# Pairs of experts: reads issued a step behind their writes, rows gathered eight tiles ahead, slots listed in another order

## The chip, the cores and the metric

The kernel runs on one core of one Trainium2 chip. TensorE (PE) multiplies matrices, VectorE (DVE) and ScalarE (ACT) work elementwise, GpSimd (POOL) does indirect gathers and some elementwise work, SyncE (SP) issues transfers. The core has 16 DMA engines, which all its queues share. The metric is the device time of one execution in microseconds (us), as the median of several runs.

## The reference

The input x is (2, 2048, 512) in fp32. The reference is, cut to what matters:

```python
xn = layernorm(x)
s  = attention(xn)            # inner layernorm, causal, one head of 512, output projection, + xn
g  = silu(moe(xn))            # below
return x + s * g

def moe(x):                   # 4096 tokens, E = 8 experts, D = 512, H = 352
    scores = x @ gate_w.T + gate_b + bias
    top_scores, top_idx = top_k(scores, 2)
    gates = softmax(top_scores)
    comb = sum(one_hot(top_idx) * gates)
    h = silu(einsum('td,ehd->teh', x, w1) + b1)
    y = einsum('teh,edh->ted', h, w2) + b2
    return einsum('ted,te->td', y, comb)
```

The kernel computes the mixture for the two chosen experts of each token alone.

## The kernel before

The kernel has four stages. First the input is normalised block by block (eight blocks of 512 tokens) and projected for attention (0 to 261 us). Between these products the routing is computed: each token gets two *slots*, and slots are sorted by expert, in tiles of 128. Then the experts run tile by tile (261 to 660 us). Attention follows (to 1123 us), and it gathers each token's two expert outputs.

**The norm.** `norm_rows` writes normalised rows (`z_all`), and multiplies them on POOL by a ratio into `z_own` (L381). `turn_rows` reads the transposed copy back and stores `z_own` to DRAM as `zu_d` (L391), from which the experts gather. `put` (L869) hangs such calls behind numbered units of the projection; `key_sums` (L508, four POOL instructions) is called at fixed units too.

**The route.** `route` makes for each slot the token that fills it: one-hot tiles (`lane`, `slot_b`, L649) are multiplied on PE, and the result `toki` is the list of tokens, one column for each tile, one row for each partition.

**A tile's way through the experts.** NS is 68 tiles, of which 66 are always run; the first 60 belong to one expert each, the last are halves of two experts. In the order of the loop the first 7 tiles run singly, then 26 pairs of one expert each (`pair_step`), then the rest singly (`experts_step`). For every tile:

1. `gather` (POOL, L999): 128 rows of `zu_d` by `toki` into one of four buffers `xs`.
2. `turn`, `to_planes` (L108): `xs` is written to DRAM in four planes of 128 columns (`xs_d`, pieces of 512 bytes).
3. `read_back`, `from_planes` (L115): the planes are read back into one of four buffers `xring`, so that partition 32j + b of it holds the column piece j of the four rows 4b to 4b + 3.
4. `join`, `turn_blocks` (L119): VectorE transposes blocks of 32x32, which makes x transposed (`xT`); its output columns are written at a step of four.
5. `up` or, for a pair, `up_pair`: the product with w1. A pair uses seven half-size products (two matmuls each) and seven VectorE adds (L1179) into `hu`; its sums of x (`x_sums`, L1153) and of w1 (`w1_sums`) are made before.
6. `send_h`: `hu` is written in planes to `h_d` and read back into `huT`; `join_h` transposes it (`ht`) and applies Silu on ScalarE (L1205).
7. `down` (L1219): the product with w2; `keep_y` copies the result to `y` (two buffers) on ScalarE and SP stores it to `y_d` (L1228).

All engines run their instructions in program order, and the order is written by hand (`manual_schedule`). In `pair_step(i)` before, tile i + 4 is written out and read back in the same step: SP issues the write, and then the read-back when the write has landed. The same holds for h: it is written after `up_pair`, and its read-back is issued at the end of the same step. POOL's queue takes the writes and read-backs of the first seven row tiles, SP's all later ones. The last 32 columns of `hu` are padding; two memsets on POOL (L1061, L1062) set it before the first row tile is written.

Of the kernel before, what the change touches and what calls it, by code (L numbers as in the profile page):

```python
# [11 lines left out]
BF16 = mybir.dt.bfloat16  # L12
# [3 lines left out]
ALU = mybir.AluOpType  # L16
# [4 lines left out]
P = 128  # L21
# [5 lines left out]
def gated_attention_moe(  # L27
# [37 lines left out]
    ND = D // P  # L65
# [10 lines left out]
    FULL = (2 * NT * P - E * HALF) // P  # L76
    NS = -(-((2 * NT * P + E * (HALF - 1)) // HALF) // 2)
    NSP = NS + NS % 2
    NM = NS - 2
# [4 lines left out]
    order = list(range(2 * PAIRS, 2 * PAIRS + AHEAD_OF_PAIRS)) + list(range(2 * PAIRS))  # L84
    order += list(range(len(order), NS))
    paired = range(AHEAD_OF_PAIRS, AHEAD_OF_PAIRS + 2 * PAIRS)
# [8 lines left out]
    Q = P // 4  # L95
# [4 lines left out]
    y_d = dram.tile([NS * P, D], F32, name="y_d")  # L100
# [12 lines left out]
    def from_planes(queue, dst, src):  # L113

        queue.dma_start(out=dst, in_=src.rearrange("n j (b i) e -> (j b) n (i e)", i=4))  # L115

    def turn_blocks(dst, src):

        nc.vector.transpose(  # L119
            dst.rearrange("p c (b i) -> p i c b", i=4),  # L120
            src.rearrange("p (i c a) -> p i c a", i=4, a=Q),
        )

    y_rows = y_d.rearrange("(n p) d -> p n d", p=P)
# [60 lines left out]
    z_all = zp.tile([P, BT, D], F32, name="z_all", bufs=1)  # L185
    z_own = zp.tile([P, BT, D], F32, name="z_own", bufs=1)
# [132 lines left out]
    kts, zts, ratios, zuts, pgs = {}, {}, {}, {}, {}  # L319
    BY_TE = 1  # L320
# [30 lines left out]
    def norm_rows(b):  # L351
        xt = xin.pop(b)
        mv, va, rs = stats.pop(b)
        for t in range(BT):
            dst, src = z_all[:, t, :], xt[:, t, :]
            if b >= BY_TE:
                dst = dst.rearrange("p (j c a) -> p c j a", j=4, c=ND)
                src = src.rearrange("p (c j a) -> p c j a", j=4, c=ND)
            nc.vector.tensor_scalar(
                dst, src, mv[:, t, 0:1], rs[:, t, 1:2], ALU.subtract, ALU.mult  # L360
            )

        ratio = sm.tile([P, BT, 1], F32, name=f"ratio_{b}", tag="ratio", bufs=4)
        nc.vector.tensor_tensor(ratio, va[:, :, 1:2], rs[:, :, 1:2], ALU.mult)
        nc.vector.tensor_tensor(ratio, ratio, rs[:, :, 0:1], ALU.mult)  # L365
        nc.vector.tensor_copy(xscale[:, ts(b, BT)], rs[:, :, 0])
        nc.vector.scalar_tensor_tensor(
            xshift[:, ts(b, BT)], mv[:, :, 0], -1.0, rs[:, :, 0], ALU.mult, ALU.mult
        )
        ratios[b] = ratio  # L370
        if b >= BY_TE:
            to_planes(nc.sync, z_d[ts(b, BT)], z_all)
        for t in range(BT):
            dst, src = z_own[:, t, :], z_all[:, t, :]
            if b < BY_TE:
                dst = dst.rearrange("p (j c a) -> p c j a", j=4, c=ND)
                src = src.rearrange("p (c j a) -> p c j a", j=4, c=ND)
                own = ratio[:, t, :].unsqueeze(2).unsqueeze(3).to_broadcast([P, ND, 4, Q])
            else:
                own = ratio[:, t, :].to_broadcast([P, D])  # L380
            nc.gpsimd.tensor_tensor(dst, src, own, ALU.mult)  # L381
        if b < 2:
            turn_rows(b)
        if b < 2:
            load(b + 2)

    def turn_rows(b):
        if b >= BY_TE:
            zuts[b] = zup.tile([P, BT, D], F32, name=f"zuT_{b}", tag="zuT")
            from_planes(nc.sync, zuts[b], z_d[ts(b, BT)])  # L390
        nc.sync.dma_start(out=zu_rows[:, ts(b, BT), :], in_=z_own)  # L391

    def keys(b):
# [97 lines left out]
    LATE = 5  # L491
# [115 lines left out]
    def route():  # L607

        with ExitStack() as rt:
# [7 lines left out]
            for e in range(E):  # L617
# [5 lines left out]
                out=tri, in_=tri, compare_op=ALU.is_ge, fill=0.0,  # L623
# [5 lines left out]
            nc.gpsimd.memset(ones, 1.0)  # L629

            def counting(name, n, step=1, cm=0, dt=F32):
                i = rp.tile([P, n], I32, name=f"{name}_i")
                nc.gpsimd.iota(i, pattern=[[step, n]], base=0, channel_multiplier=cm)
                f = rp.tile([P, n], dt, name=name)
                nc.vector.tensor_copy(f, i)
                return f
# [9 lines left out]
            half = rp.tile([P, NJ], F32, name="half")  # L646
            nc.vector.tensor_copy(half, half_i)

            lane = counting("lane", P, dt=BF16)  # L649
            slot_b = counting("slot_b", NSP, dt=BF16)  # L650
            tok = [counting("row", NT, step=0, cm=1, dt=BF16), counting("tile", NT, dt=BF16)]

# [216 lines left out]
    def put(i, f, *args):  # L869
        between.setdefault(i, []).append((f, args))  # L870
# [5 lines left out]
    for b in range(1, NB):  # L876
        at = begin[b]
        put(at, keys, b)
        put(at + 3, both, b)
        put(at + (4 if b == NB - 1 else 7), keep_scores, b)  # L880
        if b > 1:

            before = begin[b - 1] if b > 2 else 0
            put(max(before - 1, 0), norm_stats, b)
            put(before + 1, norm_roots, b)
            put(before + 1, norm_rows, b)
            put(before + 3, turn_rows, b)
            if b + 2 < NB:

                put(before + 4, load, b + 2)  # L890
# [102 lines left out]
    xhp = st.enter_context(tc.tile_pool(name="xhp", bufs=1))  # L993
    xs = xsp.tile([P, 4, D], F32, name="xs")
    xring = xhp.tile([P, 4, D], F32, name="xring")
    FIRST = 6

    def gather(i):
        nc.gpsimd.indirect_dma_start(  # L999
            out=xs[:, (i + 1) % 4, :], out_offset=None, in_=zu_d,  # L1000
            in_offset=bass.IndirectOffsetOnAxis(ap=toki[:, order[i] : order[i] + 1], axis=0),
        )
# [49 lines left out]
    NHU = 4  # L1052
# [5 lines left out]

    hu = htp.tile([P, NHU, NH * P], F32, name="hu")
    huT = htp.tile([P, NHU, 4 * NH * Q], F32, name="huT")  # L1060
    nc.gpsimd.memset(hu[:, :, H:], 0.0)  # L1061
    nc.gpsimd.memset(hu[:, :, H : H + 1], 1.0)  # L1062
    xts, phs, hts, experts = {}, {}, {}, {}

    def slots(i, n=1):
# [4 lines left out]
    def turn(i, n=1):  # L1070
        queue = nc.gpsimd if i < paired.start else nc.sync
        to_planes(queue, xs_d[i : i + n], xs[:, slots(i, n), :])
        written.append((queue, xring[:, slots(i, n), :], xs_d[i : i + n]))
# [3 lines left out]
    def read_back(which, but=0):  # L1077
        while len(which) > but:
            from_planes(*which.pop(0))

    def join(i):
        xT = xtp.tile([P, ND, P], F32, name=f"xT_{i}", tag="xT")
        turn_blocks(xT, xring[:, (i + 1) % 4, :])
        xts[i] = xT

    def places(i):
# [112 lines left out]

    def join_h(i):  # L1200
        ht = hp.tile([P, NH, P], F32, name=f"ht_{i}", tag="ht")
        turn_blocks(ht, huT[:, (i + 1) % NHU, :])
        for c, (h0, hn) in enumerate(HCH):
            for at, j in places(i):
                nc.scalar.activation(  # L1205
                    ht[:hn, c, at], ht[:hn, c, at], AF.Silu, bias=b1sel[:hn, c, j : j + 1]
                )
        hts[i] = ht
# [16 lines left out]
    def keep_y(i, copy=nc.vector.tensor_copy):  # L1225
        y = yp.tile([P, D], F32, name=f"y_{i}", tag="y")
        copy(y, pys.pop(i))
        nc.sync.dma_start(out=y_rows[:, order[i], :], in_=y)  # L1228

    pys = {}  # L1230

# [2 lines left out]
    def experts_step(i):  # L1234


        def at(f, k):
            if 0 <= i + k < NM:
                f(i + k)

        if i != NM:
            at(copy_w2, -DOWN)
        if 0 <= i - DOWN - 1 < NM:
            keep_y(i - DOWN - 1, *[nc.scalar.copy] * (i < paired.start))
        at(turn, 4)
        if i + FIRST >= 4:
            at(gather, FIRST)
        read_back(written, i + 4 < NM)
        if i + 1 not in xts:
            at(join, 1)  # L1250

        for _ in range((2, 2, 1, 4, 3, 3, 1)[i] if 0 <= i < paired.start else 0):
            w1_sums(*sums_left.pop(0))
        if i < FULL:
            at(join_h, -2)
        at(up, 0)
        at(copy_w1, 1)
        at(send_h, 0)
        if i >= FULL:

            at(join_h, -2)
        at(down, -DOWN)
        read_back(written_h, i < NM)
# [4 lines left out]

    def pair_step(i):

        keep_y(i - DOWN - 1, nc.scalar.copy)
        read_back(written_h)
        read_back(written)
        turn(i + 4, 2)
        for k in range(2):
            gather(i + FIRST + k)
        if i > paired.start:
            join_x(i + 2)
        up_pair(i)
        if i == paired.start:  # L1280

            join_x(i + 2)
        read_back(written)
        send_h(i, 2)
        for k in range(2):
            join_h(i - 2 + k)
        down(i - DOWN)
        keep_y(i - DOWN, nc.scalar.copy)
        down(i - DOWN + 1)
        read_back(written_h)  # L1290
        if i + 2 in paired:
            x_sums(i + 2)

# [132 lines left out]
        mx, nm, pieces = scored[s]  # L1426
        nc.vector.tensor_reduce(nm, mx[:, : len(pieces)], AX.X, ALU.max, negate=True)

    for i in range(-5, 0):
        experts_step(i)  # L1430
        for _ in range(min(2, len(units) - 1) if i < -1 else len(units)):
            next(projected)
            if w2_left:
                load_w2(w2_left.pop(0))
# [534 lines left out]
```

## Time and profile before

| | |
|---|---|
| median of 3 runs | 1127.32 us (1126.23 to 1129.54) |
| profiled execution | 1124.87 us, its span 1123.2 us |
| PE busy | 1038.8 us (92% of the span) |
| VectorE busy | 721.0 us (64%) |
| ScalarE busy, POOL busy | 374.7 us (33%), 338.7 us (30%) |
| DMA | 224,500 packets, 261.78 MB, mean 233 GB/s |
| the 24 steps of pairs from 319.8 to 600.9 us | PE busy 242.18 us of 281.1; DMA share 0.81 |

A group of the profile is a source line with its engine and operands, the number of its instructions, their busy time and mean duration, and how long the engine stood idle just before them and for whom. A stretch of the trace is given with the busy time of each engine in it, the granted TensorE clock (1.00 is full speed) and the share of time in which the 16 DMA engines were busy. A DMA queue's row has packets, MB, and the time its packets took as a share of 16 engines. "A <- B" among the waits means that A stood until B was done. Line numbers are those of the kernel before.

### The profile page before, as it was taken

What the parts mean: (1) busy time and instruction counts of PE and PEld (TensorE: products, weight loads), DVE (VectorE), ACT (ScalarE), POOL (GpSimd) and SP (SyncE); (2) the same over time, 40 slices, a digit from 0 to 9 for tenths busy, and PEclk for the clock granted to TensorE, in tenths of its full rate; (3) what the DMA queues carried; (4) which work ended last, traced back from release to release, by engine and by line L of the source; (5) the groups of instructions that cost most, each with busy time, mean ns of one, the idle gap of its engine ahead of it and who ended that gap; (6) DMA issues with size and microseconds to landing.
All of it is one profiled execution on the core that took longest, in us unless ns stands there. A gap on an engine that the chain in (4) does not pass through costs nothing. (4 is left out here: it accounts for less than half of the span.)

```text
span 1123.2 us, 12952 instructions
## 1 busy us (share of the span) xinstructions
PE 1038.8 (92%) x3924; PEld 678.4 (60%) x3924; DVE 721.0 (64%) x1397; ACT 374.7 (33%) x751; POOL 338.7 (30%) x337
## 2 busy tenths in 40 slices
PE   9999899997689879888888899999999999999998
PEld 6878687853365655655555344667766544445677
DVE  6965846992666566565664355866767654677667
ACT  3434353321222223223222341223244544433341
POOL 3352552016111211111111102222334765743312
PEclk9999999999999999999999899999999999999999
DMA  8599888859677877787878865845476876865461
GB/s 292 197 308 347 298 291 317 278 173 326 203 233 246 237 241 243 240 258 226 266 246 241 248 210 201 264 135 188 163 228 204 305 227 212 259 191 189 144 211 38
DMA packets 224500, 261.78 MB, mean 233 GB/s; under 512 B 57384, under 2 KB 154408, under 8 KB 224432
## 3 DMA queue, kind: packets, MB, share of 16 engines
q1 hardware_dynamic: 167920, 189.36, 53.5%
q0 software_dynamic: 13920, 45.62, 11.8%
q10 hardware_dynamic: 42592, 25.96, 7.5%
q8 instruction: 34, 0.56, 0.2%
q14 instruction: 34, 0.28, 0.1%
HBM read 146.46 MB, written 114.43 MB: 232 GB/s over the span
## 5 line engine op out<-in xcount | busy, mean ns | idle before, releaser
L1219 PE MATMUL py<-arena,ht 128*128 (+3 forms) x396 | 189.2, 627 | 0.0
L999 POOL DMA_INDIRECT xs<-zu_d,toki x66 | 65.9, 999 | 336.5 <-DMA xs_d<-xs 270.5
L1205 ACT ACTIVATE ht<-ht,b1sel 128x128 f32<-128x128 f32 (+3 forms) x216 | 65.6, 380 | 265.1 <-DVE ht L119 265.1
L1336 PE MATMUL ps<-k,q 128*128 128x512 f32 (+3 forms) x416 | 143.0, 495 | 0.3 <-PEq L1487 0.3
L119 DVE STREAM_TRANSPOSE xT<-xring 128x512 f32<-128x512 f32 x66 | 67.1, 1077 | 100.9 <-DMA xring<-xs_d 100.9
L1219 PEld LDWEIGHTS py<-arena,ht 128*128 128x128 f32 (+3 forms) x396 | 76.8, 198 | 87.0 <-issue 85.7
L1706 POOL DMA_INDIRECT yg<-y_d,posi x64 | 69.3, 1083 | 187.4 <-DVE yg L1717 172.5
L1336 PEld LDWEIGHTS ps<-k,q 128*128 128x128 f32 x416 | 74.6, 190 | 67.2 <-issue 55.1
L119 DVE STREAM_TRANSPOSE ht<-huT 128x384 f32<-128x384 f32 x66 | 53.0, 863 | 57.6 <-DMA huT<-h_d 56.0
L1172 PE MATMUL p<-w1s,xT 128*128 x208 | 44.7, 340 | 41.0 <-DVE hu L1179 41.0
L119 DVE STREAM_TRANSPOSE pT<-puT 128x512 f32<-128x512 f32 (+2 forms) x74 | 67.9, 979 | 13.9 <-DMA puT<-p_d 13.7
L1563 PE MATMUL po<-v,pT 128*128 128x512 f32 x152 | 68.1, 594 | 2.9 <-DVE pT L119 2.5
L381 POOL TENSOR_TENSOR z_own<-z_all,ratio 128x512 f32<-128x512 f32 x32 | 41.7, 1332 | 89.8 <-DVE ratio L365 89.8
L1172 PEld LDWEIGHTS p<-w1s,xT 128*128 128x128 f32 x208 | 33.8, 198 | 47.7 <-DVE hu L1179 47.7
L1179 DVE TENSOR_TENSOR hu<-p,hu 128x176 f32<-128x176 f32 x182 | 54.6, 334 | 9.4 <-PE p L1172 2.8
L119 DVE STREAM_TRANSPOSE zT<-zuT 128x512 f32<-128x512 f32 x28 | 27.4, 1116 | 44.4 <-DMA zuT<-z_d 33.2
L1524 ACT ACTIVATE pT<-pT,nm 128x1024 f32<-128x1024 f32 x14 | 16.1, 1148 | 114.8 <-DVE ri L1687 65.3
L1524 ACT ACTIVATE pT<-ps,nm 128x512 f32<-128x512 f32 (+3 forms) x52 | 30.7, 589 | 70.9 <-DVE ri L1687 43.9
L1735 POOL TENSOR_TENSOR o<-o,yg 128x512 f32<-128x512 f32 x30 | 39.0, 1299 | 44.3 <-DVE o L1727 43.7
L1120 PE MATMUL ph<-w,xT 128*128 (+1 forms) x112 | 41.3, 517 | 11.2 <-DVE xT L119 6.3
L1727 DVE SCALAR_TENSOR_TENSOR o<-xo,xscale,o 128x512 f32<-128x512 f32 x30 | 30.2, 1015 | 32.5 <-ACT o L1724 26.3
L1563 PEld LDWEIGHTS po<-v,pT 128*128 128x128 f32 x152 | 28.4, 190 | 35.6 <-issue 34.1
(340 smaller groups left out, 2018.5 us busy)
## 6 DMA issues: line engine op xcount, KB each, us to landing
y_d<-y SPq DMA_DIRECT2D x66, 256.0 KB
xs_d<-xs SPq DMA_DIRECT2D x26, 512.0 KB
xring<-xs_d SPq DMA_DIRECT2D x26, 512.0 KB
h_d<-hu SPq DMA_DIRECT2D x26, 384.0 KB
huT<-h_d SPq DMA_DIRECT2D x26, 384.0 KB
zu_d<-z_own SPq DMA_DIRECT2D x8, 1024.0 KB
kt_d<-kT SPq DMA_DIRECT2D x16, 512.0 KB
q<-qt_d SPq DMA_DIRECT2D x32, 256.0 KB
```

Source lines behind the costliest of these rows:

```text
L119: nc.vector.transpose(dst.rearrange("p c (b i) -> p i c b", i=4), src.rearrange("p (i c a) -> p i c a", i=4, a=Q),)
L381: nc.gpsimd.tensor_tensor(dst, src, own, ALU.mult)
L999: nc.gpsimd.indirect_dma_start(out=xs[:, (i + 1) % 4, :], out_offset=None, in_=zu_d, in_offset=bass.IndirectOffsetOnAxis(ap=toki[:, order[ ...
L1120: nc.tensor.matmul(ph[at, :], lhsT=xT[:, c, at], rhs=rhs[k], start=(c == 0), stop=(c == ND - 1),)
L1172: nc.tensor.matmul(ps, lhsT=x[:, c], rhs=y(c).rearrange("p o h -> p (o h)"), start=(c == 0), stop=(c == ND // 2 - 1),)
L1179: nc.vector.tensor_tensor(out, x, y, ALU.add)
L1205: nc.scalar.activation(ht[:hn, c, at], ht[:hn, c, at], AF.Silu, bias=b1sel[:hn, c, j : j + 1])
L1219: nc.tensor.matmul(py[at, :], lhsT=ht[:k, c, at], rhs=rhs[n], start=(c == 0), stop=(c == NH - 1),)
L1336: nc.tensor.matmul(ps[:, :w], lhsT=aqs[seq[s] // 2][:, c, ts(t % 2, P)], rhs=aks[first + j][:, c, :w], start=(c == 0), stop=(c == ND - 1),)
L1524: nc.scalar.activation(dst, src, AF.Exp, bias=nm, accum_out=rs[:, j : j + 1])
L1563: nc.tensor.matmul(dst, lhsT=turned[s][:, ts(k, P)], rhs=avs[first + k // BT][:, k % BT, cols], start=(start and k == k0), stop=(k == k1 - 1),
L1706: nc.gpsimd.indirect_dma_start(out=y, out_offset=None, in_=y_d, in_offset=bass.IndirectOffsetOnAxis(ap=posi[k][:, n : n + 1], axis=0),)
```

## The change

- **Reads behind writes.** `pair_step` now begins with the read-backs: that of the pair of row tiles written in the step before, and that of the h written in the step before. The read-backs after `up_pair` and at the end of the step are gone. Rows are written out six tiles ahead (`SENT`) instead of four, and gathered eight ahead (`FIRST`) instead of six. The single steps read rows back before they write the next tile. The loop before the first tile starts one step earlier.
- **Slots in the planes' order.** `lane` is listed so that partition 4a + i of a gathered tile holds slot a + 32i of the tile. `turn_blocks` then writes its columns in contiguous runs ("i b"), and x transposed still has its slots in order. For the 60 tiles of one expert h is turned the same way, so that the rows of y come out permuted, and the store of y puts them back: its destination is 4 x 32 rows of 512 where it was 128 rows.
- **Padding later.** The two memsets of the padding stand behind the POOL work of the last step ahead of the first tile.
- **The norm's own rows.** The multiplication on POOL and the store of `z_own` are functions of their own. For all blocks but the sixth (b = LATE = 5) they are called where they were; for that block the multiplication comes two units later, behind `key_sums(3)`, and the store two units later.

```diff
-    def turn_blocks(dst, src):
+    def turn_blocks(dst, src, rows="b i"):
...
-            dst.rearrange("p c (b i) -> p i c b", i=4),
+            dst.rearrange(f"p c ({rows}) -> p i c b", i=4),
...
             put(before + 3, turn_rows, b)
+            put(before + (3 if b == LATE else 1), own_rows, b)
+            put(before + (5 if b == LATE else 3), store_rows, b)
...
-            lane = counting("lane", P, dt=BF16)
+            lane = counting("lane", [[1, Q], [Q, 4]], dt=BF16)
...
-    FIRST = 6
+    FIRST, SENT = 8, 6
...
-    nc.gpsimd.memset(hu[:, :, H:], 0.0)
-    nc.gpsimd.memset(hu[:, :, H : H + 1], 1.0)
...
-        turn_blocks(xT, xring[:, (i + 1) % 4, :])
+        turn_blocks(xT, xring[:, (i + 1) % 4, :], "i b")
...
-        turn_blocks(ht, huT[:, (i + 1) % NHU, :])
+        turn_blocks(ht, huT[:, (i + 1) % NHU, :], "i b" if i < FULL else "b i")
...
-        nc.sync.dma_start(out=y_rows[:, order[i], :], in_=y)
+        rows = y_d[ts(order[i], P)]
+        nc.sync.dma_start(
+            out=rows.rearrange("(b i) d -> i b d", i=4) if i < FULL else rows, in_=y
+        )
...
-        at(turn, 4)
+        if i == paired.stop:
+            read_back(written_h)
+        read_back(written, i < paired.stop + 2)
+        at(turn, SENT)
         if i + FIRST >= 4:
             at(gather, FIRST)
-        read_back(written, i + 4 < NM)
...
     def pair_step(i):
 
+        read_back(written)
+        read_back(written_h)
         keep_y(i - DOWN - 1, nc.scalar.copy)
-        read_back(written_h)
-        read_back(written)
-        turn(i + 4, 2)
-        for k in range(2):
-            gather(i + FIRST + k)
+        turn(i + SENT, 2)
+        for k in range(i + FIRST, min(i + FIRST + 2, NM)):
+            gather(k)
...
             join_x(i + 2)
-        read_back(written)
         send_h(i, 2)
...
         down(i - DOWN + 1)
-        read_back(written_h)
...
-    for i in range(-5, 0):
+    for i in range(-SENT, 0):
         experts_step(i)
+        if i == -1:
+            nc.gpsimd.memset(hu[:, :, H:], 0.0)
+            nc.gpsimd.memset(hu[:, :, H : H + 1], 1.0)
```

More of the change, by code (lines that the diff above doesn't have):

```diff
@@ L372, in norm_rows @@
             to_planes(nc.sync, z_d[ts(b, BT)], z_all)
[L373 to L381, printed above, removed]
         if b < 2:
+            own_rows(b)
             turn_rows(b)
+            store_rows(b)
         if b < 2:
@@ L390, in turn_rows, with own_rows, store_rows @@
             from_planes(nc.sync, zuts[b], z_d[ts(b, BT)])
+    def own_rows(b):
+        for t in range(BT):
+            dst, src = z_own[:, t, :], z_all[:, t, :]
+            if b < BY_TE:
+                dst = dst.rearrange("p (j c a) -> p c j a", j=4, c=ND)
+                src = src.rearrange("p (c j a) -> p c j a", j=4, c=ND)
+                own = ratios[b][:, t, :].unsqueeze(2).unsqueeze(3).to_broadcast([P, ND, 4, Q])
+            else:
+                own = ratios[b][:, t, :].to_broadcast([P, D])
+            nc.gpsimd.tensor_tensor(dst, src, own, ALU.mult)
+    def store_rows(b):
         nc.sync.dma_start(out=zu_rows[:, ts(b, BT), :], in_=z_own)
@@ L631, in counting @@
             def counting(name, n, step=1, cm=0, dt=F32):
+                pattern = n if isinstance(n, list) else [[step, n]]
+                n = math.prod(size for _, size in pattern)
                 i = rp.tile([P, n], I32, name=f"{name}_i")
-                nc.gpsimd.iota(i, pattern=[[step, n]], base=0, channel_multiplier=cm)
+                nc.gpsimd.iota(i, pattern=pattern, base=0, channel_multiplier=cm)
                 f = rp.tile([P, n], dt, name=name)
```

## The prediction, made before the result was known

> **What bounds the kernel now.** I read the windows by stage first, then the waits of the stage that the change rewrites, then its DMA. The steady paired stage runs from the first product of the second pair (319.8 us) to that of the last (600.9 us): 24 equal steps in 281.1 us, 11.71 us each.
>
> ```profile
> 319.80:600.90 281.10, 242.18 (x962) 160.17 (x961) 166.79 (x361) 75.19 (x217) 45.78 (x47) 0.96 0.81 247
> ```
>
> The columns are length, busy us (and count) of PE, PEld, DVE, ACT, POOL, granted clock, DMA share, GB/s. PE is busy 242.18/24 = 10.09 us of each step, so 1.62 us per step is PE idle; the DMA engines are busy 81% of it. Who waits for whom in that stage (total us, times, longest):
>
> ```profile
> POOL xs L999 <- DMA xs_d<-xs: 236.2, 25, 10.8
> ...
> DVE xT L119 <- DMA xring<-xs_d: 79.8, 24, 4.5
> ...
> PE p L1172 <- DVE hu L1179: 38.9, 22, 3.1
> ```
> ```profile
> SPq L115 <- DMA xs_d<-xs: 111.1, 24, 5.6
> SPq L115 <- DMA h_d<-hu: 97.2, 24, 5.5
> ```
>
> The chain is plain. SP issues the write of a pair's rows and then stands 111.1/24 = 4.6 us for it before the read-back; the read-back lands late for the VectorE transposes (3.3 us per step); the adds L1179 are queued behind those transposes, and PE's last product waits for them, 38.9/24 = 1.62 us, which is all of PE's idle time. POOL's 236 us is slack, since nothing waits for it. Attention behind this stage is bound by PE (98% busy from 800 to 900 us), so what the paired stage loses or gains arrives at the end in full.
>
> **The change, part by part.** *Reads behind writes.* Read-backs move to the start of the next step and rows are written out six tiles ahead, not four. SP no longer stands for the write, and the 3.3 us on VectorE and 1.62 us on PE go. Taken alone that leaves PE's 10.09 us against 9.5 us of DMA (below), so a step of 10.1: 25 x (10.1 - 11.71) = -40 us (25 steps, since the first is set otherwise, below).
>
> *The store of y.* Its destination is now 4 x 32 rows instead of 128. No row of the trace shows a store of that shape. First its present price, from a stretch in which only y is stored:
>
> ```profile
> DMA packets 476, 0.88 MB, mean 98 GB/s; under 512 B 48, under 2 KB 48, under 8 KB 475
> ...
> q1 hardware_dynamic: 475, 0.87, 25.2%
> ```
>
> This is 671 to 680 us: 25.2% of 16 engines x 9 us = 36.3 us of engine time for 0.87 MB, that is 3.3 stores of 0.262 MB: 10.9 us of engine time each, or 0.68 us on each of 16 engines. Now the rule that speaks against this change: the Trainium skill, "DMA: Bandwidth & Descriptors", section "Why a DMA increments its semaphore by 16 and not by 1", says that a DMA runs on the largest number of engines, up to 16, that divides the slowest dimension of both sides, and on the lowest-numbered ones. With 128 and 4 that is four, always the same. This case's trace supports the counting: SP issues 560 DMAs, and its queue holds 8,840 four-byte completion packets. 552 x 16 + 8 x 1 = 8,840, and exactly eight of the DMAs (L989) have one row. By the rule a store costs 10.9/4 = 2.73 us on each of four engines; by the present row 0.68 us on all. The stretch of the 24 steps:
>
> ```profile
> q1 hardware_dynamic: 69852, 56.56, 69.3%
> q0 software_dynamic: 3840, 12.59, 11.6%
> ...
> y_d<-y SPq DMA_DIRECT2D x48, 256.0 KB
> ```
>
> With 0.3% of instruction fetch, 81.2% of 11.71 us is 9.51 us per engine and step. Two stores are 1.37 us of it, and become 5.47 us on four engines: 9.51 - 1.37 + 5.47 = 13.6 us. That is the upper end, because mean packet times hold the long reads, some of which run side by side on an engine. With the median packet times of the trace (ns: 22 for the 384 B pieces of h_d, 27 for the 512 B pieces of xs_d, 65 for huT, 84 for the 2 KB rows of xring and y, 160 for the gathers) an engine of the four does per step 64 x 22 + 64 x 27 + 16 x 65 + 16 x 84 + 64 x 84 + 8 x 160 ns, 12.2 us, and with the completions 12.25, the lower end. I take the middle, 12.9 us, because both ends describe the same traffic. This exceeds PE's 10.1, so four engines set the step: 25 x (12.9 - 11.71) = **+30 us** (+13.5 to +47). By the 16-engine row it would be the -40 above.
>
> The waits that this adds: SP issues the read of h only when the write of h has landed, with a store of y and the next write of rows queued behind it, and ScalarE's copy into y waits for the store two before (two buffers), with the copy of the first product and the Silus behind it. Both feed the same loaded engines later; they make no step longer than the engines' own sum as long as work is queued there, and SP has a whole step of it queued.
>
> *Slot order and transposes.* The permuted list (L649) costs the same iota (0.23 us) in the route. The transposes write contiguously instead of at a step of four. Now:
>
> ```profile
> L119 DVE STREAM_TRANSPOSE xT<-xring 128x512 f32<-128x512 f32 x66 | 67.1, 1077 | 100.9 <-DMA xring<-xs_d 100.9
> ```
>
> The bounds are 1.08 us as now and 0.68 us, what a TENSOR_TENSOR of 128x512 takes (L423). VectorE is busy 166.79/24 = 6.9 us of a step, so PE and DMA hide either value; I take no change. Were VectorE the bound, the difference would be up to 1.4 us a step.
>
> *Start of the experts.* The padding's memsets stood 7.5 us on POOL, ahead of the first write of rows:
>
> ```profile
> 252.82 0.21 POOL L1061 MEMSET hu<- 128x128 f32 x1 [7.53 <-DVE share L859]
> ```
>
> The first row tiles come 5 to 7 us earlier, and PE's idle 4.84 us before the first expert (265.61) goes. This does not reach the first pair, though. It waits for the sums of x, which stand behind the fifth ht transpose on VectorE; those transposes start at 281.54, 287.60, 293.85, 300.08 and 306.48, one per 6.2 us: transpose 0.86, Silus 0.99, copy of hu 0.43, issues 0.8, landing some 3.1. That ring is not edited; its head hangs on the weight loads ahead on SP (last at 270.30, waiting for stores of v). I take -1 us (-3 to +2, the latter if the first 4-engine stores cross it). Gathering eight ahead adds no instruction, only moves 66 of 1.0 us on an idle POOL.
>
> *Block 5 of the norm.* Its own-scaled rows (4 x 1.25 us on POOL) move behind the key sums of block 3, for which PE waits once:
>
> ```profile
> PE bank_d L554 <- POOL arena L513: 3.3, 1, 3.3
> ```
>
> PE has no other gap there: -3 us. The 1 MB store of those rows also moves two units later on SP, past the four loads of x and the store of q. Those loads then land sooner and the rows are gathered over 100 us later. Its price lies in z_own: block 6's rows (136.29 us) need that store landed. Issued near 129 with some 6.5 us to land, it is at the edge: 0 to +3 us, so this part is -3.3 to 0.
>
> *Behind the pairs* the tiles still storing through four engines share them with the loads of k; 614 to 660 us already has a DMA share of 0.86. Six such stores add 2 us each on four engines; PE's work hides most of it: +2 us (0 to +6).
>
> **Sum.** +30 - 1 - 3 + 2 = +28 us on the profiled execution's 1124.87 us (span 1123.2 and 1.67 around it): 1152.9. The median of the runs, 1127.32, lies 2.45 above that execution: 1155.
>
> **Rivals.** (1) The store still runs on 16 engines. For it: the same 128 rows of 2 KB move, and every large DMA of the trace does. Against it: the completion count, which follows the number of rows. Then PE bounds: -40 - 1 - 3 = -44, so 1083. This is the faster side. It is decided by one number: below about 11.7 us of work per step on the busiest engine the stage gains, and that is reached if a store has at least six to eight engines. (2) Four engines, but their packets overlap so well that they finish a step in the present 11.7 us (84 ns for 2 KB would have to fall towards 75): the lost and won waits cancel, and -4 from the start remains: 1123. (3) Four engines, with mean packet times or pauses in their queues (SP held by the h write while they run dry): 13.6 us a step, some 1172 to 1182.
>
> **How the numbers follow.** Four engines as the bound (with rival 3 as its upper part): 0.83, own range 1134 to 1182 (13.5 - 3 - 3.3 = +7, and 47 + 2 + 6 = +55). Rival 1: 0.12. Rival 2: 0.05. The range leaves out rival 1 and the far tails: 1120 to 1182. The three runs spread by 0.3%, about what can be told from no change. Faster: rival 1, half of rival 2 and the lowest tail, 0.15; same 0.04; slower 0.81.
>
> **What the profile after would show.** If right: DMA packets in all fall by 60 stores x 12 completions = 720 from 224,500; a store of y takes longer to land than its present 3.5 to 7.7 us; steps of about 12.9 us; DMA share in the stage falls to about 0.74 while the step grows; SP's waits for xs_d are gone, and PE's waits move to what the late h or x reads feed. If the memset mattered more, the first pair starts well before 301.9 us. The prediction is wrong if the packet count is unchanged, or if a step falls under 11 us.

## The result, and the profile after

The changed kernel takes 1224.55 us (median of 3 runs, 1221.99 to 1226.66) against 1127.32 before: a ratio of 1.086, 95% interval 1.082 to 1.090. Slower, as forecast, but by 97 us where +28 was forecast, and 43 us above the upper end of the range.

Where the time went, by the starts of PE's products (us, from the two traces):

| stretch | before | after | difference | forecast |
|---|---|---|---|---|
| start to the first product of the second pair | 319.8 | 323.3 | +3.4 | -4 |
| 24 steps of pairs | 281.1 (11.71 each) | 364.3 (15.18 each) | +83.2 | +28.6 |
| last pair to the end of the span | 522.4 | 535.3 | +12.9 | +2, and +1.2 for a 25th step |
| span | 1123.2 | 1222.8 | +99.6 | |

The paired stage once more, now of the kernel after. The columns are those of the prediction's first line: length, busy us (and count) of PE, PEld, DVE, ACT, POOL, granted clock, DMA share, GB/s.

```profile
323.27:687.53 364.26, 278.25 (x961) 202.90 (x960) 140.97 (x353) 70.13 (x209) 45.47 (x48) 0.84 0.66 189
```

PE is busy for 76% of the stretch where it was busy for 86%, and the DMA engines for 0.66 instead of 0.81. So this is not a stage in which the sixteen are full. The waits of the same stretch (total us, times, longest), first the engines', then SP's queue from 319.8 to 688.6 us:

```profile
DVE ht L119 <- DMA huT<-h_d: 172.8, 23, 8.6
...
PE p L1180 <- DVE xs L1161: 86.0, 23, 4.9
```
```profile
SPq L1237 <- ACT y L1235: 120.1, 24, 9.2
SPq L115 <- DMA h_d<-hu: 22.6, 24, 1.2
SPq L115 <- DMA xs_d<-xs: 12.1, 24, 0.7
SPq L108 <- DVE hu L1187: 9.8, 13, 1.2
```

SP's wait for the write of rows has gone from 4.6 us a step to 0.5, as the prediction said. In its place SP stands 120.1/24 = 5.0 us for ScalarE's copy into y. VectorE waits 172.8/23 = 7.5 us a step for the read of h (26.6 us in all before), and PE 86.0/23 = 3.7 us for the sums of x, which follow the h transposes on VectorE.

The packets of the whole kernel after:

```profile
DMA packets 223780, 261.77 MB, mean 214 GB/s; under 512 B 56664, under 2 KB 153688, under 8 KB 223712
```

224,500 - 223,780 = 720, that is 60 stores x 12 completions: by this count the stores run on four engines. What a step looks like on SP (start, us it took, operation):

```profile
446.00 0.52 SPq L1237 DMA_DIRECT2D y_d<-y  x1
447.02 0.36 SPq L115 DMA_DIRECT2D xring<-xs_d  x1
448.39 0.36 SPq L115 DMA_DIRECT2D huT<-h_d  x1
448.85 0.54 SPq L1237 DMA_DIRECT2D y_d<-y  x1
449.50 0.96 SPq L108 DMA_DIRECT2D xs_d<-xs  x1
451.39 6.23 SPq L108 DMA_DIRECT2D h_d<-hu  x1
461.38 0.52 SPq L1237 DMA_DIRECT2D y_d<-y  x1
```

Two things are to be seen. The order is store, two read-backs, store, two writes, so every read and every write is issued behind a store that uses the same four engines. And SP took 6.2 us to issue the write of h (median of the stage 6.5), for which it took 0.46 us before:

```profile
448.63 0.46 SPq L108 DMA_DIRECT2D h_d<-hu  x1
```

The transfers of that step, in 40 slices of 0.4 us from 447 to 463 us (upper line: busy tenths of the sixteen engines):

```profile
DMA  2356199853679467989999986544999821113113
GB/s 61 52 45 36 46 297 369 323 210 77 116 116 160 145 195 268 312 310 275 289 320 352 357 296 239 197 156 145 305 296 286 236 88 60 44 44 84 42 51 66
```

At both ends of the step there are some 2 to 3 us with mostly 36 to 66 GB/s. In the trace's packet records 2 KB packets on one engine start 80 ns apart, 1.5 KB ones 61, 512 B ones 23.4 and 384 B ones 18.7, which is 20 to 26 GB/s an engine: about two engines work there, and fourteen have nothing. From 460.6 us on most packets are 512 B ones, 34 in each 0.4 us, and then 384 B ones, some 42, which is two engines' pace: the last pieces of the two writes that SP waits for.

The transposes, last:

```profile
L119 DVE STREAM_TRANSPOSE ht<-huT 128x384 f32<-128x384 f32 x66 | 36.7, 587 | 239.5 <-DMA huT<-h_d 239.5
...
L119 DVE STREAM_TRANSPOSE xT<-xring 128x512 f32<-128x512 f32 x66 | 43.4, 687 | 13.3 <-DMA xring<-xs_d 13.3
```

1077 has become 687 ns and 863 has become 587, by writing contiguously.

### The profile page after: what moved, and what is told of

It is laid out like the page before. It is cut to its first block, busy times and chain, and to the rows that moved or that the text cites. A ratio compares the mean times of both kernels' runs of the same rounds, so it can differ in the third digit from the quotient of the medians.

```text
span 1222.8 us, 12954 instructions
## 1 busy us (share of the span) xinstructions
PE 1078.5 (88%) x3924; PEld 724.2 (59%) x3924; DVE 688.7 (56%) x1397; ACT 371.9 (30%) x751; POOL 335.9 (27%) x337
## 2 busy tenths in 40 slices
DMA packets 223780, 261.77 MB, mean 214 GB/s; under 512 B 56664, under 2 KB 153688, under 8 KB 223712
## 5 line engine op out<-in xcount | busy, mean ns | idle before, releaser
L1227 PE MATMUL py<-arena,ht 128*128 (+3 forms) x396 | 179.2, 598 | 1.6 <-ACT ht L1213 1.6
L119 DVE STREAM_TRANSPOSE ht<-huT 128x384 f32<-128x384 f32 x66 | 36.7, 587 | 239.5 <-DMA huT<-h_d 239.5
L1180 PE MATMUL p<-w1s,xs 128*128 x208 | 69.5, 483 | 96.9 <-DVE xs L1161 96.9
L1227 PEld LDWEIGHTS py<-arena,ht 128*128 128x128 f32 (+3 forms) x396 | 72.1, 187 | 79.0 <-issue 75.6
L1180 PEld LDWEIGHTS p<-w1s,xs 128*128 128x128 f32 x208 | 56.0, 310 | 103.6 <-DVE xs L1161 94.5
L1187 DVE TENSOR_TENSOR hu<-p,hu 128x176 f32<-128x176 f32 x182 | 59.1, 339 | 47.6 <-PE p L1180 44.5
L1180 PE MATMUL p<-w1s,xT 128*128 x208 | 56.9, 413 | 0.0
L119 DVE STREAM_TRANSPOSE zT<-zuT 128x512 f32<-128x512 f32 x28 | 27.3, 1110 | 45.4 <-DMA zuT<-z_d 40.7
L119 DVE STREAM_TRANSPOSE xT<-xring 128x512 f32<-128x512 f32 x66 | 43.4, 687 | 13.3 <-DMA xring<-xs_d 13.3
```

The lines of the kernel that those rows point to most:

```text
L119: nc.vector.transpose(dst.rearrange(f"p c ({rows}) -> p i c b", i=4), src.rearrange("p (i c a) -> p i c a", i=4, a=Q),)
L1180: nc.tensor.matmul(ps, lhsT=x[:, c], rhs=y(c).rearrange("p o h -> p (o h)"), start=(c == 0), stop=(c == ND // 2 - 1),)
L1187: nc.vector.tensor_tensor(out, x, y, ALU.add)
L1227: nc.tensor.matmul(py[at, :], lhsT=ht[:k, c, at], rhs=rhs[n], start=(c == 0), stop=(c == NH - 1),)
```

## The experiments

Every ratio is to the kernel before, run on the same chip beside it. "Step" is the median distance between SP's issues of two reads of xring in the trace; by that measure it is 11.59 us before and 15.29 after. The kernel before had medians of 1125 to 1132 us on the chips used, so a difference in us between two other kernels is good to some us only.

The expectations weigh explanations by name. *Work*: the engines that carry a store have more to move than a step has time for. *Ring*, or *turn*: a step is a closed chain of waits (read of h, transposes, Silus, copy, store, read of h). *Form*: a strided store is dear in itself. *Queue*: transfers that somebody waits for are issued behind stores. In y_16, y_8, y_2, late_8 and turn_two_2 the rows of y land in another order within their tile, so these kernels leave out the reference's row order; the bytes moved are the same.

| kernel | engines per store | us | ratio (95%) | step, us |
|---|---|---|---|---|
| before | 16 | 1127.32 | 1 | 11.59 |
| after | 4 | 1224.55 | 1.086 (1.082 to 1.090) | 15.29 |
| y_rows | 16, plain rows | 1105.78 | 0.980 (0.975 to 0.986) | 10.47 |
| y_16 | 16 | 1126.26 | 0.999 (0.997 to 1.001) | 11.48 |
| y_8 | 8 | 1172.28 | 1.038 (1.034 to 1.041) | 13.53 |
| y_2 | 2 | 1270.79 | 1.126 (1.122 to 1.130) | 16.50 |
| before_y4 | 4 | 1217.41 | 1.081 (1.076 to 1.086) | 15.01 |
| late_store | 4 | 1205.14 | 1.071 (1.067 to 1.076) | 14.46 |
| late_8 | 8 | 1126.68 | 1.002 (1.000 to 1.003) | 11.78 |
| rows_late | 16, plain rows | 1114.83 | 0.990 (0.987 to 0.993) | 11.19 |
| act_y | 4 | 1196.00 | 1.060 (1.054 to 1.066) | 14.40 |
| act_rows | 16, plain rows | 1099.80 | 0.980 (0.974 to 0.985) | 10.22 |
| turn_two | 4 | 1229.68 | 1.087 (1.079 to 1.094) | 15.37 |
| turn_two_2 | 2 | 1273.08 | 1.126 (1.118 to 1.133) | 16.50 |
| y_last | 4 | 1156.75 | 1.027 (1.023 to 1.031) | 12.60 |
| last_rows | 16, plain rows | 1087.88 | 0.965 (0.960 to 0.970) | 9.78 |
| bufs_4 | 4 | 1224.16 | 1.089 (1.083 to 1.095) | 15.25 |

### How many engines a store has

Four kernels differ from the changed one in the store's shape alone. y_rows turns h back to the rows' own order, so that a store is 128 plain rows:

```
-        turn_blocks(ht, huT[:, (i + 1) % NHU, :], "i b" if i < FULL else "b i")
+        turn_blocks(ht, huT[:, (i + 1) % NHU, :])
...
-        nc.sync.dma_start(
-            out=rows.rearrange("(b i) d -> i b d", i=4) if i < FULL else rows, in_=y
-        )
+        nc.sync.dma_start(out=rows, in_=y)
```

> The change with one part undone: h is turned in its old order, so y comes out in order and is stored to 128 rows as before. Theory of work (the engines that carry a store of y do more per step than anything else; a step after the change is 15.18 us, of which two stores on four engines are 5.45 us): two stores on 16 engines are 1.36 us, the DMA falls to 9.5 to 11.1 us a step and PE's 10.1 us becomes the bound: 1083 to 1125 us, and PE's waits for x or h mostly gone. Theory of the ring (the read of h is issued behind a store whose copy waits for the Silus of the read before; only half of the stores lie in it): the step falls by 2.04 us, 1172 us.

y_16, y_8 and y_2 change one figure (here y_16):

```
-            out=rows.rearrange("(b i) d -> i b d", i=4) if i < FULL else rows, in_=y
+            out=rows.rearrange("(b i) d -> i b d", i=16) if i < FULL else rows, in_=y
```

> The store keeps its strided, three-dimensional destination, but with 16 x 8 rows instead of 4 x 32 (so rows of y land in another order within their tile, and the output differs). Theory of work: as with 128 rows, 1083 to 1125 us. Theory of the ring: 1172 us. Theory of the form (a strided destination is dear in itself, whatever its outermost size): 1225 us, no change.

> The destination has 8 x 16 rows (order within the tile differs, and so the output). Completion packets rise by 60 x 4 = 240 against the changed kernel. Theory of work: two stores on eight engines are 2.73 us a step, 15.18 - 2.73 = 12.45 us, some 1157 us. Theory of the ring: half of that, 1190 us. Theory of the form: 1225 us.

> The destination has 2 x 64 rows (order within the tile differs, and so the output). Theory of work: two stores on two engines are 10.9 us a step, 15.18 + 5.45 = 20.6 us, some 1360 us. Theory of the ring: half of that, 1292 us. Theory of the form: 1225 us.

The packet counts are 224,500 for 16, 224,020 for 8, 223,780 for 4 and 223,660 for 2, so by the completions the number of engines follows i. y_rows lies in the range that *work* gave, y_16 just above it, y_8 between *work* (1157) and *ring* (1190), y_2 under both (1360 and 1292). The store's shape explains the whole loss: without it the change is 2% faster than before. Two parts can be told apart. The number of engines costs 1224.55 - 1126.26 = 98 us from 16 to 4. The strided form costs 1126.26 - 1105.78 = 20 us at the same 16 engines and the same bytes, although y_rows has the slower transposes of h; SP took 0.53 us to issue it where the plain one took 0.33.

The sizes fit no simple theory. By count, a store's work per engine doubles with each halving, but the losses are 46, 52 and 46 us. With two engines, one step takes 16.50 us, and two engines' work at the packets' pace is 128 x 80 ns for two stores and 64 x 18.7 + 64 x 23.4 + 16 x 61 + 16 x 80 + 8 x 160 ns = 6.2 us for the rest, 16.5 us: that fits two engines that are simply full. With four, the same count gives 5.1 + 6.2 = 11.4 us, and the step is 15.3. Something beside the work counts.

### The store alone, in the kernel before

```
-        turn_blocks(ht, huT[:, (i + 1) % NHU, :])
+        turn_blocks(ht, huT[:, (i + 1) % NHU, :], "i b" if i < FULL else "b i")
...
-        nc.sync.dma_start(out=y_rows[:, order[i], :], in_=y)
+        rows = y_d[ts(order[i], P)]
+        nc.sync.dma_start(
+            out=rows.rearrange("(b i) d -> i b d", i=4) if i < FULL else rows, in_=y
+        )
```

> The kernel before with nothing but its y store changed to 4 x 32 rows on four engines (and the transposes of h to the slot order that this needs). In it the write of a pair's rows and the read-backs stand behind its y stores too, and SP stands for that write. Work theory (engines' own sum, as in the prediction): 12.25 to 13.6 us a step, 1141 to 1175 us. Ring theory: two stores stand in the serial turn of the step and each is some 2 us longer on four engines, 25 x 4.1 = 102 us more: some 1230 us, about what the whole change costs, so the new order of the read-backs would not be to blame for the loss, only the store.

before_y4 takes 1217.41 us, nearer to *ring* (1230) than to *work* (at most 1175), so the store by itself costs the old kernel nearly what the whole change costs. Its SP waits, from 400 to 580 us (12 steps), and its issues of the write of h (min, median and max in ns):

```profile
SPq L115 <- DMA xs_d<-xs: 94.1, 12, 8.1
SPq L115 <- DMA h_d<-hu: 48.2, 12, 4.3
```
```profile
L108 SPq DMA_DIRECT2D h_d<-hu x23: 451/462/747, 337.2 to 669.1; - x23
```

SP waits 94.1/12 = 7.8 us a step for the write of rows, where it waited 4.6 with the old store, and 4.0 as before for the write of h. In that kernel's order the write of rows is issued right behind a store, and it lands 3.2 us later; by the prediction's count the store itself is 2.05 us longer. SP issues the write of h in 0.46 us here, and the loss is nearly the same, so long issues are not needed for it. The new order of reads and writes is not what made the change slow; it didn't save it either.

### The second store behind the next read-backs

In late_store, the store whose copy stands behind the Silus is held back in a list and issued behind the next step's two reads; rows_late is the same with plain rows, late_8 the same with eight engines.

```
...
     def pair_step(i):
         read_back(written)
         read_back(written_h)
+        store_held()
         keep_y(i - DOWN - 1, nc.scalar.copy)
...
-        keep_y(i - DOWN, nc.scalar.copy)
+        keep_y(i - DOWN, nc.scalar.copy, hold=True)
```

> The changed kernel, with one order of issue changed: the second y store of a step (the one whose copy on ScalarE stands behind that step's Silus) is held and issued at the start of the next step's work behind that step's two read-backs, so SP no longer stands for the copy ahead of the reads. The stores still run on four engines and every transfer is the same. Ring theory (the step of 15.2 us is the serial turn read of h, transposes, Silus, copies, y store, read of h): the turn is broken, the step falls to what the four engines need by themselves, 12.25 to 13.6 us, that is some 1162 to 1185 us in all. Work theory (the four engines need 15.2 us a step): unchanged, 1225.

> The kernel with 128-row y stores (y_rows, step 10.96 us, 1105.8 us) with the same late issue of the second y store. Ring theory: its step was still 0.9 us over PE's 10.1, because SP stands 8 us for the copy ahead of the reads; broken, the step is PE's, 10.1 us, 25 x 0.86 = 21 us less: some 1083 to 1088 us, the fastest of all. Work theory: unchanged, 1106.

> The late issue of the second y store with stores on eight engines (8 x 16 rows; the rows of a tile land in another order within it). The prediction's rival 1 said that eight engines would be enough for a gain; with the store ahead of the reads eight gave 1172 us. Ring theory: with the turn broken the engines' own sum counts, 9.5 (median packet times) to 10.9 us a step (means), so PE's 10.1 or little more: some 1083 to 1110 us. Work theory: unchanged from the 1172 with eight engines.

None came out as either theory had it. With four engines 19 us came back, with eight 46, and with plain rows 9 were lost. The waits of late_store from 400 to 580 us (12 steps), SP's and one of ScalarE's, show where the time is:

```profile
SPq L115 <- DMA xs_d<-xs: 65.1, 12, 7.2
SPq L108 <- DVE xs L1161: 57.8, 10, 6.9
SPq L115 <- DMA h_d<-hu: 12.8, 13, 1.0
```
```profile
ACT y L1237 <- DMA y_d<-y: 25.4, 16, 2.9
```

SP no longer stands for the copy, but now 65.1/12 = 5.4 us for the write of rows. That write is now issued behind both stores, and the next reads wait for it. With plain rows the same wait is 87.8/15 = 5.9 us. One wait was exchanged for another. With four engines a second one came: ScalarE stood 25.4/12 = 2.1 us a step for the store two before, since there are two y buffers. So late_store doesn't show the late store alone.

### The stores in a queue of their own

```
-        nc.sync.dma_start(
+        (nc.scalar if paired.start <= i < paired.stop else nc.sync).dma_start(
```

> The changed kernel, with the y stores of the paired stage issued by ScalarE from its own queue, right behind its copy, instead of by SP. Same 4 x 32 rows on the same four engines, same transfers. Two things go: SP no longer stands behind ScalarE's copy, and the writes of rows and of h, and the read-backs behind them, no longer stand in line behind the stores in SP's queue. Turn theory (the step is a serial turn: the stores drain through four engines, the writes drain behind them in the same queue, SP waits for the writes, reads back, and only then come the next stores): the step falls towards the engines' own sum, 11.4 us (2 KB packets leave 80 ns apart on an engine, 512 B ones 23.4, so 64 x 80 for two stores and some 6.2 for the rest) to 13.6: some 1128 to 1182 us. Work theory (four engines really need 15 us a step, wherever the stores are issued): 1225 within 10.

> The kernel with 128-row y stores (1105.8 us, step 10.8 to 11) with the y stores of the paired stage issued by ScalarE. If standing behind the copy and behind the stores in SP's queue is what holds its step over PE's 10.1 us, it falls to about 10.1 to 10.3: 1085 to 1092 us. If the remaining 0.9 us are the reads of one step behind the writes of the last, whatever is ahead of them (the late issue of the second store made it slower, not faster, 1114.8), it stays at 1106 within 8.

act_y takes 1196.00 us: 29 us less, and still above what the turn theory allows. The DMA queues of act_y from 400 to 580 us (packets, MB, share of 16 engines); q10 is ScalarE's, and holds nothing but stores of y there:

```profile
q1 hardware_dynamic: 33691, 23.68, 45.8%
...
q10 hardware_dynamic: 3418, 6.79, 11.1%
...
y_d<-y ACTq DMA_DIRECT2D x26, 256.0 KB
```

11.1% of 16 engines x 180 us is 320 us for 6.79/0.262 = 25.9 stores: 12.3 us each, 3.09 us on each of four engines, against the 2.73 of the prediction. A recorded packet time can be far longer than the distance of two starts (2 KB in the changed kernel: mean 112 ns, median 84, and 80 from start to start), so this is not all work. SP waits 99.4/13 = 7.6 us a step for the write of rows here: in a queue of their own the stores still run on those four engines, and the writes still finish late. ScalarE stood for a y buffer here too (15.4 us in 13 steps). In act_rows, with plain rows, the step fell to 10.22 us as the first reading in its expectation said, but only 6 us of the total followed, within the intervals of both.

### Is the turn through the transposes and Silus the limit?

By now the theory was that a step is the four engines' 11.4 us and some 4 us of a turn in which they have little to move. Doubling a part of that turn, with no DMA added, tests it:

```
-        turn_blocks(ht, huT[:, (i + 1) % NHU, :], "i b" if i < FULL else "b i")
+        for _ in range(2 if paired.start <= i < paired.stop else 1):
+            turn_blocks(ht, huT[:, (i + 1) % NHU, :], "i b" if i < FULL else "b i")
```

> The changed kernel with every h transpose of the paired stage done twice (0.587 us each, so 1.17 us more VectorE work a step, with no DMA added). VectorE is busy under half of a step, so this is hidden unless it lies in a serial turn. Sum theory (the step is the four engines' own work, 11.4 us at 2 KB every 80 ns, plus some 4 us of a turn in which they have little to move: read of h lands, transposes, Silus, copy, store): the step grows by about 1.2 us, 25 to 29 us in all, to some 1250 to 1255 us. Work theory (the four engines are busy all through the 15.2 us): no change, 1225 within 6.

> The same doubling in the kernel with stores on two engines (1270.8 us; 2 x 64 rows, so the rows of a tile land in another order within it), as a control. Its two engines' own work is 128 x 80 ns for two stores and 6.2 us for the rest, 16.5 us, and its step is 16.5 us: they never run dry. Both theories: the turn is hidden there, 1271 within 8. If it also grows by 25 us or more, the turn counts there too, and the step isn't the engines' work even with two.

The turn theory falls: 1229.68 us, a ratio of 1.087 (1.079 to 1.094) where the changed kernel has 1.086. Waits of turn_two from 400 to 580 us (12 steps):

```profile
DVE ht L119 <- DMA huT<-h_d: 72.6, 12, 6.8
```
```profile
SPq L1238 <- ACT y L1236: 69.7, 12, 8.6
```

SP stood longer for the copy (5.8 us instead of 5.0), and the read of h, issued later, was waited for less (6.1 us instead of 7.5). So the read doesn't take a fixed time from its issue. It behaves as if it landed when what is ahead of it on the slowest of its engines has drained; that is argued from these two waits. turn_two_2 takes 1273.08 us where y_2 took 1270.79, with the same step of 16.50 us, as both theories had it.

### The stores behind the writes

So the stores had to go from ahead of the other transfers. In y_last both stores of a step are issued last, behind the writes of rows and of h; it has four y buffers, and bufs_4 has those alone. last_rows is y_last with plain rows.

```
...
     def pair_step(i):
...
-        keep_y(i - DOWN - 1, nc.scalar.copy)
+        keep_y(i - DOWN - 1, nc.scalar.copy, hold=True)
...
         send_h(i, 2)
+        store_held()
...
-        keep_y(i - DOWN, nc.scalar.copy)
+        keep_y(i - DOWN, nc.scalar.copy, hold=True)
...
-    yp = st.enter_context(tc.tile_pool(name="yp", bufs=2))
+    yp = st.enter_context(tc.tile_pool(name="yp", bufs=4))
```

> The changed kernel with both y stores of a step issued last, behind the writes of rows and of h, and four y buffers in place of two. Same 4 x 32 rows on the same four engines. Now the writes that SP waits for before its read-backs don't stand in the engines' queues behind this step's stores, and the stores drain while those waits last. Queue theory (the missing 1.7 to 2.9 us of a step are the writes and reads that stand in the four engines' queues behind stores, with SP waiting for them while the engines run empty): the step falls under the 14.3 to 14.6 us of the other two orders, to 11.4 (packets at 80 ns per 2 KB) to 13.6: some 1128 to 1182 us in all. Work theory (two stores of 3.07 us each on four engines, as the act_y run shows in its own queue, and 8.1 us of the rest: 14.3 us): no lower than 14.3, 1195 or more.

> The changed kernel with four y buffers in place of two, and its order of issue kept: the control for y_last. ScalarE's copies wait for no store in the changed kernel's trace, so both theories: 1225 within 6. If it falls by more, the prediction's wait 'for the store two before' costs time after all.

> The same order and four buffers with 128-row stores on 16 engines (y_rows: 1105.8 us, step 10.8). The stores are cheap there, and the reads of the next step would stand only 1.3 us behind them: queue theory: between 1090 and 1110, step 10.2 to 10.8. Work theory: 1106 within 8.

y_last takes 1156.75 us: 68 us of the 97 are back, with the same stores on the same four engines (the step 12.60 us). bufs_4, at 1224.16 us, shows that four buffers by themselves bring nothing; y_last with two wasn't run. Its order also takes away SP's wait for ScalarE's copy, so the 68 us belong to both, the wait and the line. SP's waits of y_last from 400 to 580 us (some 14 steps), and one step of its issues:

```profile
SPq L108 <- DVE hu L1187: 39.9, 14, 4.6
SPq L115 <- DMA h_d<-hu: 14.0, 15, 1.0
SPq L115 <- DMA xs_d<-xs: 9.0, 14, 0.8
```
```profile
449.87 0.36 SPq L115 DMA_DIRECT2D xring<-xs_d  x1
451.23 0.36 SPq L115 DMA_DIRECT2D huT<-h_d  x1
451.70 0.64 SPq L108 DMA_DIRECT2D xs_d<-xs  x1
454.51 0.63 SPq L108 DMA_DIRECT2D h_d<-hu  x1
455.19 6.99 SPq L1246 DMA_DIRECT2D y_d<-y  x2
```

What SP waits for now is mostly the sum into hu (2.9 us a step), less the transfers (0.6 and 1.0), and its long issues are those of stores, which nobody waits for. The transfers from 447 to 463 us:

```profile
DMA  7522222419966986994879999999999632222234
GB/s 213 165 88 85 84 84 80 67 51 106 148 154 241 404 328 236 205 218 152 252 287 376 406 389 355 370 342 323 350 338 303 204 118 93 87 85 85 83 89 61
```

The tail in which only a few engines work is still there, 2 to 3 us mostly at 80 to 93 GB/s. But that is four engines at the pace of small packets; in the changed kernel it was about two, at half the rate. Why two of the four ran behind the others there isn't settled; the records don't name the engine.

last_rows takes 1087.88 us, ratio 0.965 (0.960 to 0.970), and is faster than both kernels. It is a little under what *queue* gave (1090 to 1110). It is the change without its new form of store, with the stores issued last and four y buffers. What SP waits for in y_rows and in last_rows (400 to 560 us, 15 and 16 steps), the longest entry of each:

```profile
SPq L1237 <- ACT y L1235: 97.9, 15, 8.0
```
```profile
SPq L108 <- DVE hu L1187: 34.7, 16, 2.8
```

## Why the prediction was wrong in size

*The store on four engines*: right. The 720 packets are gone, and the store's new shape is the whole of the loss (y_rows 1106, before_y4 1217). The 3.5 to 7.7 us that the prediction gives for the landing of a store are those of the gathers of y (yg <- y_d, median 5.3); the traces have no landing for SP's stores, so that sign can't be read.

*The engines' own sum, 12.9 us a step*: near for another order than the one it was made for. y_last has steps of 12.60 us and takes 1156.75 us, and the forecast was 12.9 and 1155. How much of this is luck is open: the packets' pace gives 11.4 us, and nothing shows that the four engines are what fills y_last's step, in which SP waits 2.9 us for the sum into hu. With two engines the count by pace and the step do agree (16.5).

*"Both feed the same loaded engines later; they make no step longer than the engines' own sum as long as work is queued there, and SP has a whole step of it queued"*: this is the step that failed. Work was queued, and its order was the harm. One store was issued ahead of the writes of rows and of h, and another ahead of the reads, on the same four engines, so transfers that somebody waits for landed behind stores that nobody waits for. At the ends of the step fourteen engines had nothing for some 2 to 3 us, while two still moved the last pieces of the writes. With the stores behind, the step fell by 15.29 - 12.60 = 2.7 us and the whole by 68 us. The two waits named just ahead of that sentence were put at nothing. SP's wait for the write of h is 22.6/24 = 0.9 us a step; ScalarE's copy doesn't wait for a store anywhere in this stage; but SP stood 5.0 us a step for that copy, with the reads behind it.

*Reads behind writes, -40 us taken alone*: the waits went as said, the size not. With plain stores it gave -22 in the order written (y_rows), where a store, and with it 97.9/15 = 6.5 us a step of SP's wait for the copy, still stood ahead of the reads. With the stores last it gave -39 (last_rows), but there the floor is another: the step is 9.78 us, under the 10.1 that the prediction took from PE's busy time. That time was at a granted clock of 0.96; from 327 to 560 us of last_rows the clock is 1.00 and PE is busy 223.76 us of 233. So the match with -40 is in part luck.

*Transposes, no change*: not contradicted. 1077 ns fell to 687, near the lower bound of 0.68, and doubling those of h moved the total by 5 us, within the intervals. That was in a kernel that waits for DMA; whether the faster transposes of x have a part in the gain of y_rows wasn't tried.

*The form of the store at sixteen engines, not priced*: wrong. It is 20 us (y_16 against y_rows). Its cause is open.

*Start, -1, and block 5, -3*: neither came. PE's idle 4.84 us ahead of the first expert went, as said, but PE stood 8.8 us for an x transpose behind it (2.9 at most before), and the second pair starts 3.4 us later instead of 1 earlier; why was not tried. PE's wait for the key sums went as well, and other waits of 1.9 to 3.3 us took its place: the projection ends 0.6 us later.

*Behind the pairs, +2 (0 to +6)*: too small; it is +12.9. The waits of after from 687 to 745 us hold these:

```profile
ACT ht L1213 <- DVE ht L119: 38.6, 5, 11.7
DVE ht L119 <- DMA huT<-h_d: 36.9, 6, 10.1
...
PE ph L1128 <- ACT w1c L1109: 11.7, 1, 11.7
```

The read of h is late here too, and ScalarE waits behind it at the Silus with a copy of weights that PE needs: 11.7 us at one place, where PE waited 4.9 for the same copy before. The single steps wait for the same reads as the pairs do; PE's work was named as their cover, and PE is behind them in the chain.

*Rival 1 (sixteen engines)* didn't happen, and its threshold was wrong too: with eight engines a store, put at "enough for a gain", the kernel is 45 us slower than before. With the second store late, eight come out even (1126.68). *Rival 2* is out. *Rival 3* named pauses in the queues, which came, at too small a price, since it stopped at 13.6 us a step; SP's long issue of the h write came too, but before_y4 lost nearly as much without it. The DMA share in the stage, named as 0.74, is 0.66.

## What to carry to other kernels

Work out the busiest engine's sum, but then go through the queue in its order: for each transfer that somebody waits for, name what stands ahead of it on its slowest engine, and add it. In this kernel a store whose destination was rearranged to an outermost size of 4 was slow for itself and for what was issued behind it; keep it at a size that all engines share (16 and 128 both ran on sixteen here), and issue stores that nobody waits for behind the writes and reads that are waited for (here 97 us of loss became 29; with plain rows the gain went from 2% to 3.5%).

## What was not expected of the hardware

SP can take long to issue a transfer: the write of h took it 0.46 us before and 6.5 us (median) after, for the same bytes, about 4 with stores on eight engines (y_8), and 0.46 again in before_y4 with stores on four. Two stores of y_last took it 6.99 us. The long issues came where stores on few engines had been issued shortly before; what sets their length is open.

Stores to 16 x 8 rows at stride cost 20 us in all over stores to 128 plain rows (y_16 against y_rows), with the same number of packets, the same bytes and the same count of completions.

A transpose on VectorE that writes at a step of four elements took 1077 ns for 512 elements and 863 for 384; contiguous ones took 687 and 587.

PE's granted clock in the paired stage was 0.96 before, 0.84 after, where PE waits longer, and 1.00 in last_rows, where PE is busy for 96%. PE's busy time for the same products rose from 242 to 278 us. How much of the longer step this carries was not measured; where PE's products reach SP, in its wait for the sum into hu, SP stood 9.8 us in all 24 steps.
